# Moving a gating product from GpSimd to VectorE, and a convolution's residual into PSUM, in a four-layer kernel

## The chip, the core and the metric

The kernel runs on one core of a Trainium2 chip. The time is the device time of one execution in microseconds (us). Five engines work side by side, each through its own queue in order: TensorE (PE in the profile, its weight loads PEld), VectorE (DVE), ScalarE (ACT), GpSimd (POOL) and SyncE (SP), which here only issues DMAs. Before the change three runs took 3255.39, 3256.88 and 3258.67 us: the median is 3256.88 us.

## The reference

Four layers follow one another on an input x of 4 images, 128 channels and 64 x 64 pixels.

```python
# layer 0: attention over the 4096 pixels of an image
energy = einsum('bnd,bdm->bnm', q, k); attn = softmax(energy, -1)
x = gamma * einsum('bcj,bij->bci', v, attn) + x
# layer 1: two quantised 3x3 convolutions with seven taps each
out = act_quant(bn_eval(conv3x3(x, wq1)))            # clip to 0..1, 16 levels
x = act_quant(bn_eval(conv3x3(out, wq2)) + x)
# layer 2: Mamba over the pixels, 256 inner channels, 16 states
xh, z = split(x @ W_in); xh = silu(causal_conv_k2(xh))
h = exp(dt * A) * h + dt * B * xh                    # per pixel, channel and state
y = sum over states of h * C + xh * D
y = (y * silu(z)) @ W_out                            # the gating
x = silu(group_norm(y)) + x
# layer 3: attention with 64 channels, softmax(k q^T) v, projection, + x
```

## The kernel before, in words

Channels lie on the 128 partitions. An image's 4096 pixels are cut into pieces of 512 (8 rows); the first piece of the first image is halved, so there are 33 pieces, 31 of 512 pixels and 2 of 256. Image after image passes layer 0 (attention, mostly PE and ACT), layer 1 (`convolutions`), layer 2 (`preparation`, `decays`, `scans`, `additions`, `output`) and layer 3 (attention again). The eight attention stages run on PE and ACT while DVE works through the scans of other images. The last stage, layer 3 of the fourth image, can start only when the scans of that image are done.

**The scans.** For one state of a piece ACT computes the decay exp(dt A) into PSUM (line 1285, one instruction for each half of the 256 channels). For two states at a time DVE multiplies dt·x by B (line 1311, operands `ud` and `b_n`, both in SBUF), runs the recurrence for each state and half as one scan instruction (line 1331), and multiplies by C (line 1348, also two SBUF operands). POOL then adds each state's result to `y` (line 1359), 16 adds to a piece. When the sixteenth is done, POOL multiplies `y` by `sz` = silu(z) (line 1363), both halves in one instruction, and `mark("gated", g)` lets PE multiply by W_out (line 1168). `sz` is written by ACT (lines 1052 and 1082) and has one buffer.

**Who may run beside whom.** Some DVE instructions are marked `port=True` and passed through `held` (line 891). `behind` (line 894) makes each POOL add or gating wait for the last held DVE instruction before it in program order; that one is called its holder here. Scans aren't held, so an add runs beside the two scans that follow a line 1311 or a line 1348.

**The second convolution.** In `convolutions` (line 914) PE sums seven taps into a PSUM tile. ACT applies scale and offset and writes SBUF (line 973). DVE adds 15 times the layer's input from `xpad` (line 977, held), limits the sum to 0..15 (line 984, held), and rounds by adding and subtracting a large constant `MAGIC` while converting to 8 bits into `x1s` (line 987, held). PE reads `x1s` for the products of the Mamba layer.

**One small PSUM bank.** `gtile` (line 276) gives out a tile of one PSUM bank; its pool has one buffer. Convolutions, projections of the Mamba layer, transposes and small sums all use it in turn. An item of work marked `bank=True` takes it, and `release()` frees it.

**The order.** Each part of the work is a Python generator. Each `yield op(...)` names the engine, a planned time and what must be done before. The class `Order` (line 188) holds one chain for each letter, and the string `SCORE`, 9949 letters long, says which chain issues its next item. So the program order on every engine is written out by hand, letter by letter. The planned times have no part in running it.

Of the kernel before, what the change touches and what calls it, by code (L numbers as in the profile page):

```python
# [74 lines left out]
    "finish3": "CDEFGHIJ",  # L75
# [4 lines left out]
ittiiuccbvaauitatiaiswjaijaiiukuiviajkajiitkwtiikjijkikcuuisjbbibjkbbittikjjidkikuujiikjibbxcjik  # L80
xxkxbajijabjikkikjjiidxkjayyyykijyieeesejkibjseeiceeceeeekfjkffkijfikffkjjiifdxfjfffxkjxffffpffk
xiixpesfkjkfeffjenlnmlnnfmniinpekfellhmjfnnknenomjoifjkfinhmnlnnmjeifkdlijenpyneylnommjkkihlneyi
eefsnjojknnnflnlhmmffopnnnnfiinkynfkkjiyomlmhjnfpnoonnojlfiknpnjflfmfnonnsmfhkldffnoffkxxnnnxlol
mfppxxnehkfiinenfffejmnnjofekiehlneofmelnjmnnonnikejieneesjflkmeikohjmlnnijpnnijlnophmmnkfflkons
nnodiynijnnyppjmylflfhmkkinjoonnifjfnolflnnnommhnnkfpffkifnnnlnfmhmjokpgonlnnifngjllnfhmfonnnfmn
nikfjffylfmlhpyfmiiokfkdonnonnnnjofkfpfhfknjisljmijfnnonkkploinmnipjjkklnonomnfiikjjhinolkjdfimj
nxnikfxfxxlpnnkxfppjxmoxkkenehenmlijonijeelnmkniijpeeokenhjlnneeeiiemknojnjlfppfnhmkpiodnjinnjfo
kkflkmnnfkflinnmnijhjponppflfmknoniinjogfjklimjgijhnnlkfnokffmndypnpijffnyyfylkkpnyymynflhiejmff
onennokkffijffieejekhkmieelnijnfeenopkinejlmjkndiikjjnloihpneiknjmpnopnklkojpinmfnjikhklnnfomnne
oijflpiknfjkisjfpmdnxjlnmnnoxhpnoiffxjxkkpiljxmiffjnnogklxxmhiisknnojgffkgpennlfefkjifnemopnnejo  # L90
limhiennkjfnpejklnpmfofdiijelnfmkknfnhjoninifjflgnjmnkkijikkjplmpohnifinnonjjkklmnfdijonyffeeffe
ipheenkkjmlnnyykypiiyyojyjffkiijkkknejelopmnnnpmklninhjoiejiipjsdelkjnnompiiknelnhmnffonklnmonnf
fejjkppnfkifpilofmnhnnjjoekflmnzffknnggglpniokotzzzmitudenuxhnelneieeoivmittpfnufuhnmlnpiiwntpit
xxolununxxmfffnflxxmopneheoffffffinnnefeepfelnimtntponeveeesieelomuuniwneefijkhnliifnojjmnijpnln
pkhomiijnneeeejlpkknmnonpkiefelmeeopjnnhfkinijjlmknnkidijmkonlnnfkffsijohljimpnnfjkijkijnoeplenh
pnffmokipljnnoofnfkiimlgnjggkmnknfpnofdyphlnnyfikmfynyoyyjmylpnnonhfnkijjfpfkflmijnonnijlkijkmnn
ophijpkeiiljfkfnmekjonnfpffldmnpoehnnnijiffekifjfpklkjnmnkiikejofnlmphnonnjkiijkjefkofldxnmnijxx
xpnijhlmnkonkiikexjnxxlmonknsijikjjippnlfkjffmennfphijoinlfnmnoefkjlmnhnpopnnofffokidigfkglfmfgp
jnnjhnmfklepoekeiifnnjnpjkelonkimnnpffielojjmkfnffhinijknlonmkdynjeklneepeiyikyyeoyhnmjpnnpyjkif
ylnfoijmkkjneielnihjnkjmiinjjolnmeeeeonnffkfffkpiednppoijjeflkkhnmienenjifkmelpjnokkiijnknjiiljm  # L100
jnhonnklkdmxnpnoijinopjlnkxxxkfmnksxfxpiixhlnnkjmfjofinejnilnjohmnepenoopkfkiiffjlkmffgnkpngeefd
kglnjiiemonhnnepjmoljnkfnfelfkijnfmfnhokifipnnkjipjlmikjfjfkonnnlmfpnfonhkdlnnfeiijmyjeokknlipim
nkpnnojikjhjeenepoilijkjnmnpffiifkffnyyjkyykiydljhmnynkokijifjkklnesjemijonnpnilnmnpfeoekeenpjol
mkiinneknjljepneomkdnxffnepeiijkofxxmfplnxjnkenffxijiopkxxmlknjineljnijpnfkmifonejilkkgmnonnnooj
fgkfmlngeeippnsdelnjmnnpikfoeijfknifjijjfflekkinmonifkfnjklmnnojpffkfnlpiimnonnfjlkndmynjeeioeek
kjlymiyyispenynppkyjjoiikkfjynfffeefnjkfilnjeemneoenkiiljemnkepndkjomlniijhnnpofnkjkilisoenmnjkk
pneofjilmfipjnjhnlnkzfkfmfonnlfpenitkpthimdnxpuxunzxonffiilnvtitxxxiexolzzuumenwimentfitugnounfi
phgngipfgvttfloiggnmniuuoplwffffijnmonghiigjjlnnpknmfnfkoiifeljenmjnnpflhonekepiimfjopnkejlnknii
pkhjmijnjelnonmeeeinoggponffggeffikkfdggkggggggeejglgnjgnkgeeesmgknggeihijkkjlngpgiinokmejknpjlg
nghkpmdnyoiiejjgenijyilkyyykmnegeeynnyfokfijjijkpnkmlnniiheofknjoffjmlnppfinenoijlmknsjfhfnnkoio  # L110
igfdjkjfpmplngkffkgfniglfmhnieefnnjonjiikelekpmoenjnknjlmhoinnpnjifkklfjmopfiidnxnjxnlnmffnjkkox
hfpknpxxxpolmfixnjnijlenphkeomnknijnifjpffkffmiljknknofnpieojeidljhmnnnijeekkkoliijkjmknnnfiflij
jpmhkkeoknnpnildnjmnyioejepnelosypynkiiykyhjmyynkjinijlfkfmjfkffnnpoeeminphoilnkejnffmklnnfjoini
ejlghnjngmnkefoedipnepeoifgslmkfojekknnnpffmeiholjennienkjjemlnfipiojnffkkpnplfhomnjnknieffflkjd
iixnmnonpkjxlxxxnojkxmnxihijjlkefnkkmenonffiifjeeppfjfehknilmknpnionejjijkdlnoijmipnnokkijlifneh
mnnkjjkoeilmeiknkfppnnfjleejsonmnifhniokjjplnfkfmdyinepnijfopljkfyfmkyyhyiinlnfmjnpoyyjneeokgnkk
fgflmgnofhnnfnilimnnjkefpejieiojlmfknnnffhokpnjlmideppiojfkkfjifnnnlnmhjniojlnfmkkiijjkninliksfp
onohmpknnnjjlmokdpnnxfffffnpeikxxxkjijleijmnknhelijoffnexmninkjkijkopnmloijnkhnpnlopkxndmiinxene
jjlnkkiimhnjjkkponepiiflkjknomnenpfjmhfslnnfoknppiijjflkfmfdnynonifljhggmnonnooijikjelyyngyeymne
pikyfyfphlkffnomfnnnelnipofffjmpnjfffehkklnnmenioepneeijlkjnmnoeisijnflkjkidnomhpnneiejjolkfkknm  # L120
nffffkiijefejempepniiplokkhnejnnjezekeflpomknzznnlniimnhvonwliopdxnviminnfwlnfxfimznfhvopenlnfmo
infwxpfifenvhxospmlnnnoofxwlgmingjijpnxxliijgnnmnjhkkkkifofppnikjlkffnmofkipjlfkfnnnhfmnonkfijif
kplnjmokifnnjjkdloidimhjpjennnmelfnkkponkkkknopifjmlhijnfeeijpennfijfflkkkfeokijmnnkkiiddpnjkplj
mehkoiiennnjklpeekknjskmioniCljnhnjiiomnjnfflmnnCkkkokkpjkldpijenifmodhnfnnppjijklomknniienfplkk
fkjmknnhonojklnfiiemknpnjkfjlinhoimnnjppjofkkkfilnmddijnjglengkkkhmnfnonpokfkkflmfpnAiinnjejlehe
mnofnnoijffflmnniiffefkppkjCilkkCChfnCpmnonnooeCkkjjCidCdfgjmklfnnkfffkijijfenhlnkkkminopjepnelo
ikjfCksknDmDniipjkkkenjliioddknjkmpnnpkijlijkjnmkflkiionnmnnjjofkknfplmnnofifjieplnfpfmonnnkjifo
kkojflgfinifpgmkgjfflnmDnonDnnDDDiDjBddilnkkomnDkkklpkmpnojjfnnnfffiljmnifnkkiffoEkEppnjlmonnkkj
pkfflndiijEndikEomjkknknilpEmoEjpiEFjnnnkkkolnFijmnfffjDAffkkinjloiEnEpmfjpnEikknkjiidldmFFkojnn
jnkoklphFmnnnkkiFFiBfjlnFjkkmnFppiiojjlnnkkipjmoinffhknflfnomnkfpjfkdlmhnffioinnnojojlgdgiimnffk  # L130
gppkkjngklggknfpfiomhnjkjnnklnffmiiffnojklkjijmnpfpfFinnAfhofnkkloGGmnnnkddjlnphmofninGGjpplnikk
kkomGkGinGjkjlGmGhijijnnnggpokknfkffkiikfkgjiddlfjkmfHoGnnHnkjlnkoihmpjijnHniiHHkkHHBookflnmpnji
jlgHjmpHnnnohgngkkgggggggpggmgiglkkfkoknnifjfpjggnifidggodlmnfgjkkfnjgkhilgmpnfgpngknoHjfkgkknfo
# [54 lines left out]
class Order:  # L188
# [5 lines left out]
    def __init__(self):  # L194
        self.marks = set()
        self.chains, self.count = {}, {}
        self.locks = {True: None, "h": None}

    @staticmethod
    def op(engine, time, *needs, bank=False, **_):  # L200
        return needs, bank
# [1696 lines left out]
```

## Time and profile before

The profile is of one execution, whose own time was 3258.73 us; the instructions span 3256.9 us of it.

| | busy, us | share of the span |
|---|---|---|
| TensorE | 3075.6 | 94% |
| VectorE | 2942.3 | 90% |
| ScalarE | 2550.4 | 78% |
| GpSimd | 1298.7 | 40% |
| line 1363, gating on POOL, 33 instructions | 75.9 | 2.3% |
| line 987, second rounding on DVE, 33 instructions | 14.5 | 0.4% |

The mean granted TensorE clock was 0.983. In a line of the groups stand the source line, the engine and the operation, the tiles written and read, the shapes and the count; then the busy time in us and the mean duration of one in ns; and after the second bar the time that the engine sat idle just before these instructions, with what ended that time. Such a duration runs from an instruction's start to its end, and on DVE and ACT the next instruction can start some hundredths of a microsecond earlier. In a line of the timeline stand the start, the length, the engine, the line, the operation and, at xN, how many such instructions were merged.

### The profile page before, as it was taken

How to read it: one execution, taken by the hardware profiler on the slowest of the kernel's cores; microseconds unless marked ns; L12 is line 12 of the kernel's file. 1: busy time of each engine (PE TensorE's matmuls, PEld its weight loads, DVE VectorE, ACT ScalarE, POOL GpSimd, SP SyncE). 2: the span in 40 equal slices, each digit the busy share in tenths (PEclk: the TensorE clock that was granted, in tenths of full speed). 3: DMA queues.
4: the chain of work that ended last, by engine and by line, in shares of the span. 5: the costliest groups of instructions: out<-in, count | busy, mean ns of one | idle time of the engine just before them, and what ended most of it. 6: DMA issues, size and time to landing. Idle time of an engine off the chain costs nothing. (4 is left out here: it accounts for less than half of the span.)

```text
span 3256.9 us, 69082 instructions
## 1 busy us (share of the span) xinstructions
PE 3075.6 (94%) x29404; PEld 2260.7 (69%) x29404; DVE 2942.3 (90%) x2377; ACT 2550.4 (78%) x3734; POOL 1298.7 (40%) x582
## 2 busy tenths in 40 slices
PE   8989989999899999999898999999899999999998
PEld 7878858888688887555556878865566555565665
DVE  3699999999999999999999999999999999993554
ACT  5888878888788887888787888878888888875554
POOL 0244444444344444444444444444444444450000
PEclk9999999999999999999999999999999999999999
DMA  2233333233333334333333222233333333330000
GB/s 71 81 99 106 102 118 104 96 108 105 108 117 103 104 102 131 105 109 117 111 130 127 99 98 93 97 125 109 104 125 114 133 114 113 119 108 11 2 11 22
DMA packets 134878, 321.67 MB, mean 99 GB/s; under 512 B 44384, under 2 KB 55072, under 8 KB 134560
## 3 DMA queue, kind: packets, MB, share of 16 engines
q1 hardware_dynamic: 134272, 316.32, 28.9%
q8 instruction: 232, 3.80, 0.5%
q10 hardware_dynamic: 288, 0.85, 0.1%
q14 instruction: 86, 0.70, 0.1%
HBM read 300.35 MB, written 16.78 MB: 97 GB/s over the span
## 5 line engine op out<-in xcount | busy, mean ns | idle before, releaser
L1359 POOL TENSOR_TENSOR y<-y,hs 128x1024 f32<-128x1024 f32 (+1 forms) x528 | 1220.0, 2311 | 1569.1 <-DVE hs L1311 644.6
L659 ACT ACTIVATE p<-e 128x1024 f32<-128x1024 f32 x1024 | 1016.4, 1019 | 183.5 <-PE e L641 161.7
L1331 DVE TENSOR_TENSOR_SCAN hs<-da,hlast,hs 128x512 f32<-128x512 f32 (+1 forms) x928 | 1124.7, 1249 | 36.6 <-ACT da L1285 15.8
L723 PE MATMUL us<-v,p 128*128 128x129 f32 x8192 | 1012.9, 280 | 23.7 <-ACT us L780 11.2
L723 PEld LDWEIGHTS us<-v,p 128*128 128x128 f32 x8192 | 964.5, 194 | 81.4 <-ACT p L659 16.8
L1285 ACT ACTIVATE da<-dt,late 128x512 f32<-128x512 f32 (+1 forms) x1056 | 705.5, 677 | 303.4 <-DVE hs L1331 292.0
L1311 DVE TENSOR_TENSOR hs<-ud,b_n 128x2048 f32<-128x2048 f32 (+1 forms) x264 | 620.0, 2348 | 6.3 <-POOL y L1359 4.2
L1348 DVE TENSOR_TENSOR hs<-hs,c_n 128x2048 f32<-128x2048 f32 (+1 forms) x264 | 590.8, 2238 | 4.5 <-DMA c_n<-bc_d 2.3
L641 PE MATMUL e<-it,v 64*128 64x256 f32 x4096 | 531.6, 396 | 21.7 <-ACT p L659 21.3
L732 PE MATMUL us<-p,v 128*32 128x256 f32 x8192 | 501.8, 383 | 4.7 <-ACT p L659 4.1
L641 PEld LDWEIGHTS e<-it,v 64*128 64x128 f32 x4096 | 373.1, 188 | 162.4 <-issue 74.8
L732 PEld LDWEIGHTS us<-p,v 128*32 128x32 f32 x8192 | 246.2, 110 | 216.5 <-issue 53.3
L641 PE MATMUL e<-it,j 64*128 64x256 f32 x2048 | 208.8, 313 | 24.5 <-ACT p L659 19.3
L641 PEld LDWEIGHTS e<-it,j 64*128 64x128 f32 x2048 | 142.7, 186 | 88.0 <-ACT p L659 31.6
L751 PE MATMUL us<-p,ones 128*32 128x256 f32 x3072 | 202.6, 381 | 0.0
L681 DVE TENSOR_TENSOR acc<-p,acc 128x1024 f32<-128x1024 f32 x96 | 117.5, 1224 | 39.3 <-ACT p L659 32.5
L751 PEld LDWEIGHTS us<-p,ones 128*32 128x32 f32 x3072 | 96.1, 110 | 72.9 <-issue 13.2
L1331 DVE TENSOR_TENSOR_SCAN hs<-da,hs 128x512 f32<-128x512 f32 (+1 forms) x128 | 133.2, 1074 | 7.0 <-ACT da L1285 4.4
L1028 PEld LDWEIGHTS <-w 128*128 128x128 bf16 x594 | 53.1, 98 | 85.8 <-issue 43.9
L1028 PE MATMUL xh<-x,w 128*128 128x512 fp8e4 (+1 forms) x396 | 94.7, 375 | 14.0 <-ACT xc L1074 6.7
L1363 POOL TENSOR_TENSOR y<-y,sz 128x1024 f32<-128x1024 f32 (+1 forms) x33 | 75.9, 2301 | 71.4 <-DVE hs L1348 54.8
L681 DVE TENSOR_TENSOR acc<-p 128x1024 f32<-128x1024 f32 x16 | 19.6, 1224 | 83.1 <-PE ss L694 44.4
(173 smaller groups left out, 2563.6 us busy)
## 6 DMA issues: line engine op xcount, KB each, us to landing
b_n<-bc_d SPq DMA_DIRECT2D x256, 512.0 KB, 3.7
c_n<-bc_d SPq DMA_DIRECT2D x256, 512.0 KB, 3.7
x_in<-in_x SPq DMA_DIRECT2D x16, 512.0 KB, 6.1
xpad<-in_x SPq DMA_DIRECT2D x32, 256.0 KB, 4.6
x_d<-yo SPq DMA_DIRECT2D x24, 256.0 KB, 2.1
x_in<-x_d SPq DMA_DIRECT2D x12, 512.0 KB, 5.1
o<-x_d SPq DMA_DIRECT2D x24, 256.0 KB, 4.0
out<-o SPq DMA_DIRECT2D x24, 256.0 KB, 4.2
```

What stands on the lines that cost most here:

```text
L641: nc.tensor.matmul(e[h][:, k % 2, k // 4, :], lhsT=jts[s][row : row + D3, col : col + P], rhs=its[s][row : row + D3, c * CB : (c + 1) * CB ...
L659: nc.scalar.activation(p, es[t][h], AF.Exp)
L681: nc.vector.tensor_add(accs[k], ps[t, h], other)
L723: nc.tensor.matmul(us[:, r, 0:VP], lhsT=ps[t, h][:, k % 2, k // 4, r * P : (r + 1) * P], rhs=vts[s][:, 8 * q + k, :], start=q == 0 and k = ...
L732: nc.tensor.matmul(us[m : m + 32, 0, :], lhsT=vts[s][:, 8 * q + k, m % D3 : m % D3 + 32], rhs=ps[t, h][:, k % 2, k // 4, :], start=q == 0 ...
L751: nc.tensor.matmul(us[32 * m : 32 * m + 32, 1, :], lhsT=ones[:, 0:32], rhs=term, start=False, stop=q == NQ - 1 and k >= len(terms) - 4,)
L1028: nc.tensor.matmul(g, lhsT=w3[:, k // len(rhs), lhs[k % len(rhs)] : lhs[k % len(rhs)] + P], rhs=x[:, rhs[k % len(rhs)]], start=(k == 0), s ...
L1285: nc.scalar.activation(da, live["in", g][0][:, h, :], AF.Exp, scale=amat[:, h, n : n + 1])
L1311: held(nc.vector.tensor_mul(hs, live["in", g][1].unsqueeze(1).to_broadcast([P, 2, 2, T]), bcs.pop(("b", k)).unsqueeze(2).to_broadcast([P, ...
L1331: nc.vector.tensor_tensor_scan(hs[:, m % 2, h, :], das.pop((m, h)), hs[:, m % 2, h, :], hlast[:, n, h : h + 1] if index[g] else 0.0, ALU.mult,
L1348: nc.vector.tensor_mul(hs, hs, bcs.pop(("c", k))[:, a:b].unsqueeze(2).to_broadcast([P, b - a, 2, T]))
L1359: behind(nc.gpsimd.tensor_tensor(y, y, hs[:, m % 2], ALU.add))
```

## The change

The gating leaves POOL. A new chain `gate` copies silu(z) with ACT into the one PSUM bank, a half of the channels at a time, and DVE multiplies that half of `y` by it, in place. So a piece has two ACT copies and two DVE products in place of one POOL product, and the bank is used in turn by both halves.

In the second convolution ACT's scale and offset are written back into the PSUM tile. DVE adds the residual from there, no longer held, and frees the bank only then. The upper bound is joined with the addition of `MAGIC` in one DVE instruction. ACT subtracts `MAGIC` with a Relu, which is also the bound at zero, and converts to 8 bits. A constant tile for the offset is filled once by POOL.

The score is a new one of 10048 letters (132 more for the gating, 33 fewer for the additions), and `finish3` has five letters in place of eight. The class `Order` takes a mark `~` that sets a flag; the score has no such mark and nothing reads the flag.

```diff
-    "finish3": "CDEFGHIJ",
+    "finish3": "CDEFG",
+    "gate": "H",
 }
 SCORE = "".join(
...
+    magic = const.tile([P, 1], F32, tag="magic", name="magic")
+    nc.gpsimd.memset(magic, -MAGIC)
...
                 g = gtile("conv")[:, 0 : n * W]
                 conv(g, rpad, wint[1], a, range(7))
                 yield op("ACT", 0.2 + 0.58 * part, who=who)
+                nc.scalar.activation(g, g, AF.Identity, bias=b2, scale=s2)
+                yield op("DVE", 0.12 + 0.57 * part, who=who)
                 t = att.tile([P, TB], F32, tag="t", name="q2", bufs=1)[:, 0 : n * W]
-                nc.scalar.activation(t, g, AF.Identity, bias=b2, scale=s2)
+                nc.vector.scalar_tensor_tensor(
+                    img(t), rows_of(xpad, a, n), LEVELS, img(g), ALU.mult, ALU.add
+                )
                 release()
-                yield op("DVE", 0.12 + 0.57 * part, port=True, who=who)
-                held(
-                    nc.vector.scalar_tensor_tensor(
-                        img(t), rows_of(xpad, a, n), LEVELS, img(t), ALU.mult, ALU.add
-                    )
-                )
                 if (a + n) % ROWS == 0:
                     mark("taken", b, block)
                 yield op("DVE", 0.1 + 0.33 * part, port=True, who=who)
-                held(nc.vector.tensor_scalar(t, t, 0.0, LEVELS, ALU.max, ALU.min))
-                yield op("DVE", 0.1 + 0.33 * part, port=True, who=who)
-                held(
-                    nc.vector.tensor_scalar(
-                        x1s[b % 2][:, 1 + a * W : 1 + (a + n) * W],
-                        t,
-                        MAGIC,
-                        MAGIC,
-                        ALU.add,
-                        ALU.subtract,
-                        saturate=False,
-                    )
+                held(nc.vector.tensor_scalar(t, t, LEVELS, MAGIC, ALU.min, ALU.add))
+                yield op("ACT", 0.2 + 0.49 * part, who=who)
+                nc.scalar.activation(
+                    x1s[b % 2][:, 1 + a * W : 1 + (a + n) * W],
+                    t,
+                    AF.Relu,
+                    bias=magic,
+                    saturate=False,
                 )
                 mark("x1", b, c)
...
             mark("add", m)
             if n == DS - 1:
-                yield op("POOL", 0.1 + 2.3 * width(g) / TB, ("sz", g))
-                behind(nc.gpsimd.tensor_tensor(y, y, live.pop(("sz", g)), ALU.mult))
-                mark("gated", g)
+                order.add(gate(g, y))
+
+    def gate(g, y):
+        part = width(g) / TB
+        for h in range(2):
+            yield op("ACT", 0.2 + 0.4 * part, ("sz", g), bank=True)
+            sz = live.pop(("sz", g)) if h == 0 else sz
+            ps = gtile("gate")[:, 0 : width(g)]
+            nc.scalar.copy(ps, sz[:, h, :])
+            yield op("DVE", 0.12 + 0.57 * part)
+            nc.vector.tensor_mul(y[:, h, :], y[:, h, :], ps)
+            release()
+        mark("gated", g)
```

## The prediction, made before the result was known

> **What bounds the kernel now.** I read the page's busy times and slices first.
>
> ```profile
> span 3256.9 us, 69082 instructions
> PE 3075.6 (94%) x29404; PEld 2260.7 (69%) x29404; DVE 2942.3 (90%) x2377; ACT 2550.4 (78%) x3734; POOL 1298.7 (40%) x582
> ...
> DVE  3699999999999999999999999999999999993554
> ACT  5888878888788887888787888878888888875554
> POOL 0244444444344444444444444444444444450000
> ```
>
> VectorE (DVE) is full from the second to the 36th slice; the last four are the final attention, which TensorE (PE) fills. The table of stretches says how full:
>
> ```profile
> 1400.00:2000.00 600.00, 561.33 (x5437) 396.94 (x5434) 578.53 (x438) 488.89 (x716) 273.54 (x117) 0.97 0.33 112
> 2600.00:2900.00 300.00, 291.83 (x3582) 179.18 (x3582) 291.98 (x202) 245.04 (x366) 149.04 (x62) 1.00 0.34 116
> ```
>
> Columns: window, length, then PE, weight loads, DVE, ACT, POOL. Summed over 160 to 2900 us, DVE idles 69 us of 2740, PE 155, ACT some 490, most of it behind scans. So a microsecond added to DVE there moves the last scan, and with it the final attention. The groups give the prices:
>
> ```profile
> L1285 ACT ACTIVATE da<-dt,late 128x512 f32<-128x512 f32 (+1 forms) x1056 | 705.5, 677 | 303.4 <-DVE hs L1331 292.0 <-DVE dt L1144 8.2
> L1363 POOL TENSOR_TENSOR y<-y,sz 128x1024 f32<-128x1024 f32 (+1 forms) x33 | 75.9, 2301 | 71.4 <-DVE hs L1348 54.8 <-DVE x L987 4.3 <-DVE hs L1311 3.2
> L977 DVE SCALAR_TENSOR_TENSOR q<-xpad,q 128x512 f32<-128x512 f32 (+1 forms) x33 | 22.1, 670 | 1.0 <-ACT q L973 1.0
> L880 DVE TENSOR_TENSOR o<-o,o 128x512 f32<-128x512 f32 x24 | 16.1, 672 | 2.0 <-PE o L876 2.0
> L987 DVE TENSOR_SCALAR x<-q 128x512 fp8e4<-128x512 f32 (+1 forms) x33 | 14.5, 439 | 0.6
> ```
>
> Last the timeline of POOL, then of DVE, a few instructions after a gating:
>
> ```profile
> 1929.44 2.35 POOL L1359 TENSOR_TENSOR y<-y,hs 128x1024 f32<-128x1024 f32 x1 [2.57 <-DVE hs L1311]
> 1934.25 4.81 POOL L1359 TENSOR_TENSOR y<-y,hs 128x1024 f32<-128x1024 f32 x2 [2.45 <-DVE hs L1348]
> ```
> ```profile
> 1931.84 2.27 DVE L1348 TENSOR_TENSOR hs<-hs,c_n 128x2048 f32<-128x2048 f32 x1
> 1934.02 2.45 DVE L1331 TENSOR_TENSOR_SCAN hs<-da,hlast,hs 128x512 f32<-128x512 f32 x2
> 1936.48 0.69 DVE L1184 BATCH_NORM_STATS2 stats<-yo 128x6 f32<-128x512 f32 x1
> 1937.09 4.12 DVE L1311 TENSOR_TENSOR hs<-ud,b_n 128x2048 f32<-128x2048 f32 x1
> ```
>
> One add (2.36) fits beside two scans (2.45). Here two adds ran behind one holder, until 1939.06, and L1311, which reads two SBUF operands, took 4.12 us in place of 2.28. A piece has 16 adds and 16 such places; the gating is a seventeenth POOL instruction, so about one place per piece gets two. Instruction by instruction: 127 full-width L1311 overlap an add and average 2.545 us, the 120 that overlap none 2.282; 64 L1348 average 2.387 against 2.268. That is 33.4 + 7.6 us; with smaller rows some 50 us of DVE's busy time is waiting for POOL, 24.6 of it in 23 places with two adds and 20.0 spread over 364 places with one.
>
> **The change, part by part.** A DVE price is the step from one start to the next in back-to-back work, about 0.08 us under the duration (L1184 above: 0.69 long, 0.61 step).
>
> *Gating, DVE.* Added: 66 multiplies, SBUF by PSUM: 62 of 128x512, 4 of half. Nearest row L880, same shape and operands: step 0.583. 62 x 0.583 + 4 x 0.35 = 37.5 us, all on the full engine. Bounds: L880 below, L977's 0.669 (two SBUF operands) above: 37.5 to 43. The trace shows seven L880 wholly under a POOL add at 0.665 us against 0.688 alone, so these don't collide.
>
> [...]
>
> *Second convolution, DVE.* The two bounds and the rounding were two tensor_scalars (L984, L987); now one. L987 goes: 31 x 0.361 + 2 x 0.2 = -11.6. L977's step 0.669 becomes the PSUM form, as L819 (0.650): -0.6. L984 turns into L950's operation (0.413 against 0.345; part of that is overlap): 0 to -2.2, take -1.0. DVE's sum: 37.5 - 11.6 - 0.6 - 1.0 = **+24.3**.
>
> *POOL.* 33 gatings go, 75.9 us. POOL is 60% idle, so that time alone is worth nothing; what counts is the seventeenth place. I followed both scores letter by letter: at full width the old one puts two POOL instructions behind one holder some 30 times, the new one 10 times. Of the 10, four have a wide DVE instruction beside the scans, which covers the second add; four have two short ones and cost 0.95 each, the mean of such places now; two have scans alone, some 2.2 (4.80 of adds less 2.45 and the start). That is 8 us against 24.6: -16.6. Places with one add beside nothing but two scans fall from 379 to 305: 20.0 x 74/379 = -4. L1311's idle time behind POOL, 4.3 in the stretch, I leave. Next in line on DVE are then the scans that wait for ACT's decay, 14.5 us in the stretch. Relief **-21**; bounds 0 (other adds collide instead) and -54 (all 50 + 4.3 goes).
>
> *ACT.* Added: 66 copies SBUF to PSUM, 62 x 0.626 (L1285's step, same direction) + 4 x 0.41 = 40.5, and 33 Relus at L952's 0.521, 16.8. L973 now writes PSUM: no row, bounds ±0.1 each, 0. The 57 us lie in ACT's 490 idle us, mostly waits for a scan; uncovered, they cost 57.
>
> *Waits.* Each multiply waits for its copy, and behind it on DVE stand scans. In the score the first multiply stands at least two scans behind the holder of the piece's last add, except in the last piece, so POOL isn't waited for. For the copy, DVE's idle time behind ACT in the long stretch gives L1139 0.08 us each (2.7/33), L533 0.46 (6.0/13): 5 to 30 us for 66. I take 0.1, nearer L1139, since 35 multiplies have another DVE instruction between copy and multiply: **+6.6**. The rounding's Relu is read by PE, a piece ahead of the scans: 0; uncovered, 33 x 0.6.
>
> *The one bank "g".* It holds every small matmul result. From first matmul to last reader it is taken 1697 of 2740 us. Copy and multiply add 66 x 1.3 = 86, the longer second convolution 33 x 0.65 = 21. Behind a matmul that waits for it PE queues energies and products. Cover: PE's 155 idle us and inputs a piece ahead. I take 0; 36 turns are followed by another user than the gating, so up to 36 x 1.3 = 47 on PE.
>
> *Order.* At every 48th step of the scan chain the new score has issued within four as many products, energies and exponentials as the old (finish3 moves a little more). Before the first scan PE has 85 items in place of 86, and exp, silu, ln and sqrt tables change 151 times against 149 (+2.6 at 1.28 on ACT, covered). So the head (first scan at 105 us, PE 31 to 40 of 40 busy) and the final attention keep their length: 0, ±8 for local shuffles. *Tail.* The last gating, 2938.0 to 2940.4 on POOL, becomes multiply, copy, multiply: 0.67 + 0.63 + 0.67 + two hand-overs, 2.1 to 2.4: 0. The constant's memset lies in the idle head of POOL.
>
> **Sum.** The profiled execution took 3258.7 (span 3256.9), 1.9 above the median. 3258.7 + 24.3 - 21 + 6.6 = 3268.6; less 1.9, **3267 us**, 0.3% slower.
>
> **Rivals.**
> 1. *The seventeenth place was worth more (faster).* If nearly all overlap goes, -45, and hand-overs cost nothing: 24.3 - 45 = -21, 3236; at two thirds of that, 3247. For it: a back-to-back pair stands some instructions after most gatings. Against: 20 of the 50 us sit in places with one add, which stay. It decides once relief exceeds 24.3 plus the waits.
> 2. *DVE stalls behind ACT's copy or bank g.* At L533's 0.46 per multiply 30 us: 3291. For it: in 31 cases copy and multiply are neighbours in the score, and a late copy holds DVE outright. Against: L1139, L977 and L1184 hardly wait for ACT.
> 3. *DVE's load doesn't set the end.* From 2600 to 2900 PE is 97% busy too; then relief and load both vanish in PE's order: 3257. Against: PE idles 155 us earlier.
>
> **How the numbers follow.** This kernel's measurement tells about 0.2%, 6.5 us: 3250.4 to 3263.4. Forecast 0.42 (own range 3257 to 3278: 0.30 slower, 0.12 same); rival 1 0.30 (0.28 faster); rival 2 0.18, all slower; rival 3 0.10 (0.06 same, the rest split evenly). Faster 0.30, same 0.20, slower 0.50. The range runs from two thirds into rival 1 (3241) to rival 2's price (3292).
>
> **What would show it.** Right: POOL near 1223 us; DVE busy up only a few us although 66 multiplies at about 0.67 and no L987 appear; L1311's mean, 2348 ns now, near 2270 (20 us over 264); few 4.8 us pairs on POOL. Wrong on the slow side: idle time before the multiply put down to ACT's copy above 10 us, or PE waiting for it at conv, z or xh. Wrong on the fast side: L1311 and L1348 both at 2.27 at full width, and DVE's idle time below 69 us in its long stretch.

## The result: faster by 0.7%, and the profile after

The changed kernel took 3233.82 us (median of four runs, 3233.17 to 3235.41), the kernel before 3256.14 (four runs, 3255.30 to 3258.67). The ratio is 0.9931, with an interval of 0.9914 to 0.9948. The forecast, 3267 us, had the wrong sign. The time also lies under the range, 7 us below its lower end. Rival 1, at 3236, came nearest. The profiled execution took 3233.38 us (span 3230.2), with a granted clock of 0.989.

Busy times and slices on the page of the kernel after:

```profile
span 3230.2 us, 69145 instructions
...
PE 3049.1 (94%) x29404; PEld 2251.7 (70%) x29404; DVE 2928.3 (91%) x2410; ACT 2602.4 (81%) x3835; POOL 1218.6 (38%) x550
...
DVE  3699999999999999999999999999999999993554
ACT  5888888888888888888787888888888888875554
POOL 0234434444434444444434444444444444450000
```

DVE has 33 instructions more than before (2410 against 2377), among them 66 products that cost 43 us. Even so its busy time is 14.0 us lower. So all its other work takes 57.2 us less than before, 14.5 of it the second rounding, which has left DVE. The shape of the slices is the old one: a full DVE, then the last attention stage.

Table of stretches, kernel before, then after (window, length, then PE, weight loads, DVE, ACT, POOL):

```profile
160.00:2900.00 2740.00, 2584.96 (x24098) 1910.46 (x24101) 2670.87 (x2022) 2244.40 (x3297) 1252.49 (x539) 0.98 0.33 111
```
```profile
160.00:2900.00 2740.00, 2584.13 (x24469) 1914.19 (x24466) 2685.35 (x2074) 2313.41 (x3422) 1190.81 (x515) 0.99 0.34 112
1400.00:2000.00 600.00, 557.95 (x5445) 398.85 (x5446) 585.67 (x453) 502.14 (x744) 259.11 (x111) 0.99 0.34 112
2600.00:2900.00 300.00, 292.47 (x3628) 180.42 (x3620) 295.65 (x211) 248.59 (x368) 140.44 (x60) 1.00 0.34 114
```

DVE's idle time from 160 to 2900 us is now 2740 - 2685.4 = 54.6 us; it was 69.1. In 1400 to 2000 it is 14.3 against 21.5, and in 2600 to 2900 it is 4.4 against 8.0.

Groups of the kernel before, then of the kernel after (busy time and mean ns of one, then the idle time just before them and what ended it):

```profile
L1311 DVE TENSOR_TENSOR hs<-ud,b_n 128x2048 f32<-128x2048 f32 (+1 forms) x264 | 620.0, 2348 | 6.3 <-POOL y L1359 4.2
L1348 DVE TENSOR_TENSOR hs<-hs,c_n 128x2048 f32<-128x2048 f32 (+1 forms) x264 | 590.8, 2238 | 4.5 <-DMA c_n<-bc_d 2.3 <-ACT hlast L1295 2.2
```

```profile
L1363 POOL TENSOR_TENSOR y<-y,hs 128x1024 f32<-128x1024 f32 (+1 forms) x528 | 1215.9, 2303 | 1688.6 <-DVE hs L1315 703.3 <-DVE hs L1352 452.4 <-DVE q L960 172.7
...
L1315 DVE TENSOR_TENSOR hs<-ud,b_n 128x2048 f32<-128x2048 f32 (+1 forms) x264 | 596.8, 2261 | 6.2 <-POOL y L1363 3.6 <-DMA b_n<-bc_d 0.2
L1352 DVE TENSOR_TENSOR hs<-hs,c_n 128x2048 f32<-128x2048 f32 (+1 forms) x264 | 585.7, 2218 | 0.7 <-DMA c_n<-bc_d 0.7
...
L1376 DVE TENSOR_TENSOR y<-y,gate 128x512 f32<-128x512 f32 (+1 forms) x66 | 43.2, 654 | 5.6 <-POOL y L1363 4.4 <-ACT gate L1374 1.1
...
L1374 ACT COPY gate<-sz 128x512 f32<-128x512 f32 (+1 forms) x66 | 37.8, 573 | 19.7 <-DVE y L1376 15.7 <-DVE rall L860 2.2 <-DVE q L985 1.5
...
L994 ACT ACTIVATE x<-q,magic 128x512 fp8e4<-128x512 f32 (+1 forms) x33 | 23.4, 709 | 8.1 <-DVE q L992 7.9
...
L985 DVE SCALAR_TENSOR_TENSOR q<-xpad,conv 128x512 f32<-128x512 f32 (+1 forms) x33 | 21.4, 649 | 2.2 <-ACT conv L982 2.2
```

L1315 is the line 1311 of before and L1352 its 1348. The mean of L1315 has fallen from 2348 ns to 2261, with the narrow ones of the half pieces counted in; at full width it fell from 2417 to 2327, and that of L1352 from 2299 to 2283. The product L1376 waited 1.1 us in all for its copy; its other wait, 4.4 us for POOL, is in the last piece. The copy itself, L1374, waited 15.7 us for the product before it, because both halves use the same bank.

Timeline of the kernel after around one product, first POOL, then DVE (start, length):

```profile
1381.70 2.35 POOL L1363 TENSOR_TENSOR y<-y,hs 128x1024 f32<-128x1024 f32 x1 [2.42 <-DVE hs L1352]
1386.85 2.37 POOL L1363 TENSOR_TENSOR y<-y,hs 128x1024 f32<-128x1024 f32 x1 [2.80 <-DVE hs L1315]
```
```profile
1379.30 2.27 DVE L1352 TENSOR_TENSOR hs<-hs,c_n 128x2048 f32<-128x2048 f32 x1
1381.48 0.68 DVE L1376 TENSOR_TENSOR y<-y,gate 128x512 f32<-128x512 f32 x1
1382.08 2.45 DVE L1335 TENSOR_TENSOR_SCAN hs<-da,hlast,hs 128x512 f32<-128x512 f32 x2
1384.44 2.27 DVE L1315 TENSOR_TENSOR hs<-ud,b_n 128x2048 f32<-128x2048 f32 x1
```

The add starts at 1381.70, just after the C product, and ends at 1384.05. Beside it lie the gating product and two scans. The next L1315 comes at 1384.44, when POOL is done, and takes 2.27 us; the 163 of full width that overlap no add take 2.278 on the mean. Before the change a L1311 behind two adds took 4.12.

**Where the time went.** I went through DVE's instructions from the first dt·x·B product to the end of the last C product, in both traces. This is called the stretch below. Busy time counts no overlap twice.

| part of the stretch, us | before | after | difference | predicted |
|---|---|---|---|---|
| gating products | 0 | 36.8 | +36.8 | +37.5 |
| second rounding on DVE | 12.8 | 0 | -12.8 | -11.6 |
| residual and bounds | | | -1.3 | -1.6 |
| dt·x·B products | 602.5 | 578.8 | -23.7 | |
| C products | 569.5 | 564.0 | -5.5 | |
| small GroupNorm instructions | | | -5.4 | |
| all others | | | -4.5 | |
| *the last four: less waiting for POOL* | | | *-39.1* | *-21* |
| DVE idle | 77.1 | 62.0 | -15.0 | +6.6 |
| length of the stretch | 2829.4 | 2798.0 | -31.4 | +9.9 |

The first dt·x·B product starts 2.5 us later, and what follows the last C product is 2.3 longer. That leaves -26.6 of the span. So two terms of the sum failed: the relief is nearly twice as large, and DVE's idle time fell where I had it rise.

### The profile page after: what moved, and what is told of

The parts are those of the page before. It is cut to its first block, busy times and chain, and to the rows that moved or that the text cites. A ratio compares the mean times of both kernels' runs of the same rounds, so it can differ in the third digit from the quotient of the medians.

```text
span 3230.2 us, 69145 instructions
## 1 busy us (share of the span) xinstructions
PE 3049.1 (94%) x29404; PEld 2251.7 (70%) x29404; DVE 2928.3 (91%) x2410; ACT 2602.4 (81%) x3835; POOL 1218.6 (38%) x550
## 3 DMA queue, kind: packets, MB, share of 16 engines
q1 hardware_dynamic: 134272, 316.32, 29.9%
## 5 line engine op out<-in xcount | busy, mean ns | idle before, releaser
L1315 DVE TENSOR_TENSOR hs<-ud,b_n 128x2048 f32<-128x2048 f32 (+1 forms) x264 | 596.8, 2261 | 6.2 <-POOL y L1363 3.6
L1352 DVE TENSOR_TENSOR hs<-hs,c_n 128x2048 f32<-128x2048 f32 (+1 forms) x264 | 585.7, 2218 | 0.7 <-DMA c_n<-bc_d 0.7
L651 PE MATMUL e<-it,v 64*128 64x256 f32 x4096 | 521.8, 392 | 12.2 <-ACT p L669 11.7
L651 PEld LDWEIGHTS e<-it,j 64*128 64x128 f32 x2048 | 141.5, 185 | 81.5 <-ACT p L669 31.6
L691 DVE TENSOR_TENSOR acc<-p,acc 128x1024 f32<-128x1024 f32 x96 | 117.6, 1225 | 40.1 <-ACT p L669 33.1
L1122 PE MATMUL dt_ps<-xd,late 128*128 128x256 f32 (+1 forms) x264 | 70.8, 391 | 8.3 <-ACT sp L1134 4.9
```

Source lines behind the costliest of these rows:

```text
L651: nc.tensor.matmul(e[h][:, k % 2, k // 4, :], lhsT=jts[s][row : row + D3, col : col + P], rhs=its[s][row : row + D3, c * CB : (c + 1) * CB ...
L691: nc.vector.tensor_add(accs[k], ps[t, h], other)
L1315: held(nc.vector.tensor_mul(hs, live["in", g][1].unsqueeze(1).to_broadcast([P, 2, 2, T]), bcs.pop(("b", k)).unsqueeze(2).to_broadcast([P, ...
L1352: nc.vector.tensor_mul(hs, hs, bcs.pop(("c", k))[:, a:b].unsqueeze(2).to_broadcast([P, b - a, 2, T]))
```

## The experiments

The kernel before was run beside each group of runs; its medians there were 3258.27, 3259.54 and 3259.39 us. Busy and idle are DVE's in the stretch, as in the table above. Spans and these two columns are of the profiled execution. The runs are on several chips, on which the median of the kernel before differs by up to 3.4 us; a difference of some us between two runs of the table, after among them, is no more certain than that.

| run | median, us | ratio to before (interval) | span | busy | idle |
|---|---|---|---|---|---|
| before | 3256.14 | | 3256.9 | 2752.4 | 77.1 |
| after | 3233.82 | 0.9931 (0.9914 to 0.9948) | 3230.2 | 2736.0 | 62.0 |
| conv_old_order | 3299.97 | 1.0132 (1.0115 to 1.0148) | 3298.4 | 2739.6 | 127.8 |
| gate_old_order | 3364.37 | 1.0329 (1.0312 to 1.0347) | 3362.5 | 2757.8 | 167.1 |
| both_old_order | 3406.68 | 1.0464 (1.0446 to 1.0482) | 3400.4 | 2746.0 | 217.4 |
| conv_old_later_relu | 3277.17 | 1.0047 (1.0030 to 1.0064) | 3278.1 | 2741.2 | 106.0 |
| both_old_later | 3380.06 | 1.0368 (1.0350 to 1.0385) | 3378.6 | 2745.3 | 198.2 |
| new_order_alone | 3322.73 | 1.0197 (1.0180 to 1.0214) | 3317.1 | 2799.8 | 85.9 |
| conv_gate_on_pool_new_order | 3274.23 | 1.0052 (1.0035 to 1.0069) | 3271.0 | 2752.2 | 84.4 |
| no_gating_old_order | 3227.05 | 0.9902 (0.9886 to 0.9919) | 3225.9 | 2714.4 | 81.5 |
| gating_left_out | 3209.57 | 0.9842 (0.9826 to 0.9859) | 3208.8 | 2707.8 | 68.7 |
| product_from_sbuf | 3247.99 | 0.9963 (0.9949 to 0.9977) | 3247.9 | 2752.8 | 62.8 |
| conv_undone_new_order | 3284.13 | 1.0076 (1.0059 to 1.0092) | 3282.5 | 2782.1 | 67.8 |
| rounding_back_on_dve | 3263.41 | 1.0014 (1.0004 to 1.0023) | 3263.2 | 2766.7 | 63.8 |

No run with the whole computation was faster than the changed kernel.

### Each part alone, in the old order

The first question was which part brought the gain. I took each part into the kernel before and kept its score, with as few letters changed as the parts need. conv_old_order has the second convolution of after. Because the bank is freed one step later there, four letters of the convolution chain stand earlier.

```diff
+                nc.scalar.activation(g, g, AF.Identity, bias=b2, scale=s2)
...
+                    img(t), rows_of(xpad, a, n), LEVELS, img(g), ALU.mult, ALU.add
...
+                held(nc.vector.tensor_scalar(t, t, LEVELS, MAGIC, ALU.min, ALU.add))
...
+                    AF.Relu,
```

> The old score with the second convolution's change alone; gating stays on POOL. Four letters of the convolution chain stand earlier, because the longer hold of the one PSUM bank would otherwise overlap its next user. If DVE's load sets the end: the rounding that leaves DVE is worth 12.8 us and the PSUM residual 0.7, so 3256 - 13.5 = 3243. If the gain of the changed kernel lies in its new score: 3256, no change. If the longer hold of the bank costs: above 3258.

Measured: 3299.97 us, ratio 1.0132 (1.0115 to 1.0148). The first two values were missed by over 40 us; the third, above 3258 if the longer hold of the bank costs, is met, though most of the time has another cause. DVE's busy time behaved as the sum says (-12.8), but its idle time rose by 50.7. The chain that ended these waits begins on ACT. Waits of ACT in conv_old_order (waiting line, releaser, us in total, times, longest):

```profile
ACT da L1287 <- DVE hs L1333: 235.1, 304, 2.8
ACT p L667 <- PE e L649: 190.5, 169, 5.1
ACT x L992 <- DVE q L990: 40.1, 16, 4.8
```

Waits of DVE in the same run:

```profile
DVE hs L1333 <- ACT da L1287: 43.2, 46, 5.7
```

L992 is the new Relu. In the old order it stands where DVE's rounding stood, so ACT's queue reaches it before DVE has done L990. For 40.1 us in 16 places ACT stands still there, with decays queued behind it. The scans' wait for those decays is 43.2 us here. In the kernel before it was 20.3:

```profile
DVE hs L1331 <- ACT da L1285: 20.3, 29, 1.7
```

gate_old_order has only the gating of after, on the chain `gate`, with its four letters a few places apart behind the last addition of a piece, and the letters of the additions moved so that each holder has one.

```diff
-                yield op("POOL", 0.1 + 2.3 * width(g) / TB, ("sz", g))
-                behind(nc.gpsimd.tensor_tensor(y, y, live.pop(("sz", g)), ALU.mult))
-                mark("gated", g)
+                order.add(gate(g, y))
```

> The old score with the gating's change alone. The adds of POOL are laid out anew by one rule, one add behind each holder where it fits, and the copies and products stand at the first places where the bank is free, two scans behind the piece's last add; all else keeps the old order. Theory 'seventeenth instruction': the products add 36.8 us to DVE, the pairs of adds go (24.6 us in the trace of before, about 4 left), and DVE's small instructions and single adds lose some 10 more: 3256 + 36.8 - 31 = 3262, between 3254 and 3268. Theory 'new score': without it the products cost their full price, 3256 + 36.8 - 0 to 5 = 3288 to 3293.

both_old_order joins the two.

> Both changes of the arithmetic under the old score, adds laid out as in the run with the gating alone, nothing searched. 'Seventeenth instruction' with the convolution's saving: 3256 + 36.8 - 13.5 - 31 = 3248, between 3240 and 3256, so at most half of the 22 us gain is the new score's. 'New score': 3256 + 36.8 - 13.5 = 3279, and the score's search is worth the whole gain and more.

Measured: 3364.37 us, 1.0329 (1.0312 to 1.0347), and 3406.68 us, 1.0464 (1.0446 to 1.0482). Every value expected was missed, by over 70 us in the first run and by over 125 in the second. In gate_old_order the sum on DVE's busy time again held: +5.4, which is +39.8 of products and -34.4 of relief. Idle time rose by 90.0, and in both_old_order by 140.3. In gate_old_order this is how ACT waited:

```profile
ACT da L1295 <- DVE hs L1341: 162.7, 217, 3.2
ACT gate L1380 <- DVE y L1382: 80.8, 30, 4.9
```

This is the second copy of a piece, waiting for the bank that the first half's product hasn't freed. And PE waited for the same bank:

```profile
PE conv L916 <- DVE y L1382: 38.4, 5, 9.9
PE z L1038 <- DVE y L1382: 29.9, 8, 9.3
```

So rival 2's mechanism (DVE behind ACT and the bank) exists, and where the copies and products stand badly it costs far more than the 30 us that I gave it. Part of that size is my placing of the four letters, which no search went over.

### The same with the stalls moved

If those waits at the head of ACT's queue are the cause, moving only these letters must give the time back. conv_old_later_relu moves the Relu's letter later in 21 of 33 cases, until some 2.4 us of planned DVE work stand between it and the step before it, or until the next user of its result or of its tile.

> The convolution's change alone under the old score, as before, but in 21 of 33 pieces the letter of the new Relu stands two to four DVE instructions later, so that ACT meets it when DVE's limit-and-add is done. Theory 'head of ACT's queue': the 51 us that DVE idled more came from ACT waiting at that Relu (40.1 us in 16 waits) with decays queued behind; they go to some 10 to 20, and the time falls from 3300 to 3253 to 3270, ACT's wait for line 990 below 10 us. Rival 'the bank is held longer': the Relu has no part in that, 3290 to 3300.

Measured: 3277.17 us, 1.0047 (1.0030 to 1.0064): 22.8 us less than conv_old_order, with nothing else changed. The wait of L992 fell from 40.1 us to 6.9. So that stall is shown, and its price is over half of the 41.7 us that the convolution's change lost in this order. The time lies between the two values expected, 3253 to 3270 and, for a bank held longer, 3290 to 3300: other waits stayed. Waits of ACT, then of PE:

```profile
ACT sz L1054 <- PE z L1030: 24.2, 17, 5.1
```
```profile
PE z L1030 <- DVE q L983: 14.3, 4, 5.5
PE sc L849 <- DVE q L983: 8.4, 2, 4.8
```

L983 is the residual, which frees the bank. PE waited for it as long in conv_old_order (13.8 and 8.3 us), so the longer hold of the bank may well be part of what is left; no run takes it away alone. The scans still waited 40.2 us for decays.

both_old_later does the same to both parts, with the second copy also later.

> Both changes under the old score, adds one to a holder, the Relu later as in the run beside it, and the second copy of a gating later too: at least 2.4 us of DVE work behind the first product where the next reader of the gated piece allows it. 'Head of ACT's queue': the 81 us that ACT stood at the copy go to some 30 and the Relu's 40 to under 10, so 3407 falls by 60 to 110, to 3297 to 3347. If only a search of the whole order helps: above 3380.

Measured: 3380.06 us, 1.0368 (1.0350 to 1.0385), only 26.6 us under both_old_order, where I had expected some 60 or more; it is just at the "above 3380" of the case in which only a new order of everything helps. Waits of ACT, first both_old_order, then both_old_later:

```profile
ACT gate L1374 <- DVE y L1376: 69.6, 30, 4.9
ACT sz L1056 <- PE z L1032: 35.9, 34, 2.5
ACT q L957 <- PE conv L916: 31.8, 19, 5.9
```
```profile
ACT sz L1056 <- PE z L1032: 58.4, 38, 4.9
ACT q L957 <- PE conv L916: 40.8, 20, 8.7
...
ACT gate L1374 <- DVE y L1376: 21.5, 16, 4.9
```

The copy's own wait fell by 48.1 us, but a copy that stands later holds the one bank later. PE then waits for it (z 43.5 to 64.8 us), and ACT waits for PE. The stall only changed its place. Moving these letters wasn't enough to bring this arithmetic into the old order; in the new one the same two instructions wait 15.7 and 7.9 us, and DVE is idle for 62.0 us in place of 198.2.

### The new order without the new arithmetic

new_order_alone turns the question round: the old code under the new score, with a POOL gating at the place of the first addition letter after a piece's sixteenth, the gating letters removed and one more addition letter for each piece.

```diff
-                order.add(gate(g, y))
+                yield op("POOL", 0.1 + 2.3 * width(g) / TB, ("sz", g))
+                behind(nc.gpsimd.tensor_tensor(y, y, live.pop(("sz", g)), ALU.mult))
+                mark("gated", g)
```

> The old arithmetic in both places under the new score, gating on POOL placed as in the run with the convolution's change alone. If the new score were the gain: below 3256. From the runs so far: gating on POOL in this order 3274, convolution undone +50 (more held instructions among the adds): 3300 to 3330.

Measured: 3322.73 us, 1.0197 (1.0180 to 1.0214), as the theory of an order that needs its arithmetic had it. Group of the dt·x·B products there:

```profile
L1319 DVE TENSOR_TENSOR hs<-ud,b_n 128x2048 f32<-128x2048 f32 (+1 forms) x264 | 627.1, 2375 | 27.1 <-POOL y L1367 24.5
```

They are longer (2375 ns) and on top of that wait 24.5 us for adds. The likely reason is that held instructions of the convolution and the seventeenth POOL instruction come where the new order has no place for them. But one number goes the other way. DVE's idle time is longer in all (85.9 us against 77.1), yet its idle time before all other instructions is 85.9 - 27.1 = 58.8 us, where before had 70.9 and after has 55.8. So if the waits before the dt·x·B products are left aside, some 12 of the 15.0 us of idle time that the change saved are also saved by the new order under the old arithmetic.

### What the gating on POOL cost

no_gating_old_order is the kernel before without its gating; the additions are spread as in gate_old_order.

```diff
-                behind(nc.gpsimd.tensor_tensor(y, y, live.pop(("sz", g)), ALU.mult))
```

> The kernel before without its gating (the output leaves out the factor silu(z)), POOL's adds laid out one to a holder, all other letters of the old score. It prices the seventeenth POOL instruction where it stood. 'Seventeenth instruction': DVE gets back what the gating with both changes alone gave back in the old order, 34 us of waits for POOL: 3258 - 34 = 3224, between 3218 and 3232. If POOL's pairs cost only what stands in their own places (24.6 us and 3): 3230. If the old order's idle time grows into the space: 3235 to 3258.

Measured: 3227.05 us, 0.9902 (0.9886 to 0.9919); expected was 3224, within 3218 to 3232. Groups:

```profile
L1321 DVE TENSOR_TENSOR hs<-ud,b_n 128x2048 f32<-128x2048 f32 (+1 forms) x264 | 597.2, 2262 | 7.7 <-POOL y L1369 5.2 <-DMA b_n<-bc_d 0.3
L1358 DVE TENSOR_TENSOR hs<-hs,c_n 128x2048 f32<-128x2048 f32 (+1 forms) x264 | 584.4, 2214 | 2.5 <-ACT hlast L1305 1.6 <-DMA c_n<-bc_d 0.8
```

2262 and 2214 ns are the means of after as well (2261, 2218). On an engine that is 60% idle, 33 instructions of 2.3 us, with the old spread of the adds, cost the kernel 31.0 us of span (3256.9 to 3225.9), and all of it as longer DVE instructions: busy fell by 38.0, idle rose by 4.4. Since the run also moved most letters of the adds, it doesn't part the gating from their old spread; no run has the new spread with the gating on POOL in the old order.

conv_gate_on_pool_new_order asks the same within the new kernel: after, with the gating back on POOL by the edit of new_order_alone.

> The changed kernel with the gating put back on POOL as one instruction, its copies and products left out of the score, and the seventeenth POOL instruction placed within the next nine adds, where the stretch without held DVE instructions is longest. 'Seventeenth instruction': DVE loses 36.8 us of products and gains pairs again in about 33 places at 0.7 to 2 us, 35 to 60 us: 3233 to 3258, L1311's mean back to 2340 ns or more. 'New score' (gain independent of the gating): 3234 - 36.8 = 3197 to 3205.

Measured: 3274.23 us, 1.0052 (1.0035 to 1.0069), 40.4 us above after and 16 above the upper value expected. Against after, 36.8 us of products go, but DVE's busy time rises by 16.2 and its idle time by 22.4:

```profile
L1313 DVE TENSOR_TENSOR hs<-ud,b_n 128x2048 f32<-128x2048 f32 (+1 forms) x264 | 620.3, 2350 | 20.3 <-POOL y L1361 16.7 <-DMA b_n<-bc_d 0.7
```

2350 ns is the mean of before again, and the wait for POOL is 16.7 us in place of 3.6. So the price of the gating on POOL depends on the order: here it is 62.2 us of span over the same kernel without a gating (gating_left_out, below).

### What the gating on DVE costs

gating_left_out takes copies and products out of the kernel after.

```diff
-            ps = gtile("gate")[:, 0 : width(g)]
-            nc.scalar.copy(ps, sz[:, h, :])
-            nc.vector.tensor_mul(y[:, h, :], y[:, h, :], ps)
```

> The changed kernel without the gating: no copies, no products, so the output leaves out the factor silu(z); score and all else kept. It prices the new products and copies where they stand. If DVE's load sets the end: -36.8 - 1.1: 3196, between 3190 and 3203. If PE, 97% busy from 2600 us on, is as much a bound: 3210 to 3225.

Measured: 3209.57 us, 0.9842 (0.9826 to 0.9859). The span is 21.4 us below after's. Busy time falls by 28.2: the products' 36.8, less 6.9 that L1315 gains in length (2261 to 2287 ns), probably since some adds have lost the product that lay beside them. Idle time rises by 6.7. The time is 7 us above the value for a bound by DVE's load (3190 to 3203) and just below the one for a PE that is as much a bound (3210 to 3225). So it doesn't decide between the two, but it does refute rival 3 as it stood, by which relief and load both vanish: 28.2 us off DVE's load moved the end by 21.4.

product_from_sbuf asks what the detour over PSUM is worth: the product reads silu(z) where it is, without copy or bank.

```diff
-            ps = gtile("gate")[:, 0 : width(g)]
-            nc.scalar.copy(ps, sz[:, h, :])
-            nc.vector.tensor_mul(y[:, h, :], y[:, h, :], ps)
+            nc.vector.tensor_mul(y[:, h, :], y[:, h, :], sz[:, h, :])
```

> The changed kernel with silu(z) read from SBUF by the same two products, at the same places, no copies and no bank. 'PSUM keeps the products out of POOL's way': DVE's 66 products then wait for adds that are under way, 31 to 46 of them overlap one, at 0.3 to 1.5 us: 3234 + 10 to 50 = 3244 to 3284. 'Copies and bank are the price of the gating': ACT saves 40 us and the bank 86, the time falls to 3215 to 3230.

Measured: 3247.99 us, 0.9963 (0.9949 to 0.9977), 14.2 us above after; the theory that PSUM keeps the product out of POOL's way had 3244 to 3284, and the one in which copies and bank are a cost 3215 to 3230.

```profile
L1374 DVE TENSOR_TENSOR y<-y,sz 128x512 f32<-128x512 f32 (+1 forms) x66 | 61.2, 927 | 4.4 <-POOL y L1363 4.4
```

The same product takes 927 ns in place of 654, because it now meets the adds. Of the 62 at full width 46 overlap an add in either kernel: from SBUF these take 1059 ns on the mean, from PSUM 671. The 16 that overlap none take 672 and 670, so SBUF is no slower by itself. In the stretch, products cost 54.6 us in place of 36.8: +17.8, the whole difference in span (17.7). Idle time is 62.8 against 62.0, though the copies, the waits for them and 66 turns of the bank are gone. So in the new order these cost DVE no idle time that shows.

### The convolution in the new order

conv_undone_new_order is after with the convolution of before: residual, bounds and rounding held on DVE.

```diff
-                held(nc.vector.tensor_scalar(t, t, LEVELS, MAGIC, ALU.min, ALU.add))
+                held(nc.vector.tensor_scalar(t, t, 0.0, LEVELS, ALU.max, ALU.min))
...
+                        MAGIC,
+                        MAGIC,
+                        ALU.add,
+                        ALU.subtract,
```

> The changed kernel with the second convolution as it was: ACT writes SBUF, the bank is free earlier, DVE adds the residual from SBUF, limits and rounds; the letters are those of the new score, the rounding on DVE where the Relu's letter is. If DVE's load sets the end: +12.8 for the rounding, +0.7 for the residual, a few us for held instructions that single adds now run into: 3234 + 15 = 3249, between 3245 and 3256. If the order fitted to the change is what counts: another 10 to 40 us of DVE idle time, 3256 to 3285.

Measured: 3284.13 us, 1.0076 (1.0059 to 1.0092), 50 us above after. That is the upper end of the second value, but not by its way, which was idle time: this rose only by 5.8, and busy time by 46.1. Groups:

```profile
L1321 DVE TENSOR_TENSOR hs<-ud,b_n 128x2048 f32<-128x2048 f32 (+1 forms) x264 | 602.8, 2284 | 11.1 <-POOL y L1369 8.6 <-DMA b_n<-bc_d 0.3
L1358 DVE TENSOR_TENSOR hs<-hs,c_n 128x2048 f32<-128x2048 f32 (+1 forms) x264 | 600.3, 2274 | 1.3 <-DMA c_n<-bc_d 1.3
...
L987 DVE SCALAR_TENSOR_TENSOR q<-xpad,q 128x512 f32<-128x512 f32 (+1 forms) x33 | 27.1, 821 | 2.2 <-ACT q L983 2.2
L997 DVE TENSOR_SCALAR x<-q 128x512 fp8e4<-128x512 f32 (+1 forms) x33 | 17.5, 529 | 0.2
```

The instruction itself costs 15.0 us in the stretch. The C products have grown by 14.6 (2218 to 2274 ns), the residual from 649 to 821 ns, the dt·x·B products by 6.2. These are held instructions. My reading is that each one more cuts a place between two holders in two, and that an add of 2.36 us doesn't fit into the halves. In the old order the same change freed little beside its own time (conv_old_order: dt·x·B products -1.5 us, C products -1.4), so this price belongs to the new order.

rounding_back_on_dve takes only the last step back: the residual stays in PSUM, but DVE subtracts MAGIC and bounds at zero, held.

```diff
-                yield op("ACT", 0.2 + 0.49 * part, who=who)
-                nc.scalar.activation(
-                    x1s[b % 2][:, 1 + a * W : 1 + (a + n) * W],
-                    t,
-                    AF.Relu,
-                    bias=magic,
+                yield op("DVE", 0.1 + 0.33 * part, port=True, who=who)
+                held(
+                    nc.vector.tensor_scalar(
...
+                        MAGIC,
+                        0.0,
+                        ALU.subtract,
+                        ALU.max,
```

> The changed kernel with the last step of the second convolution on DVE: the residual stays in PSUM and not held, but subtracting the constant and the bound at zero are a held tensor_scalar at the Relu's letter. Undoing both halves cost 50 us, 20 in instructions and 26 in waits for POOL. If holders that cut up the adds' places are the cause, and both held instructions share in it: +13 for the instruction and 8 to 15 of waits, 3255 to 3262. If the residual alone did it: 3247. If the rounding alone did it: 3270 to 3280.

Measured: 3263.41 us, 1.0014 (1.0004 to 1.0023), just above the 3255 to 3262 of the theory of holders, and 30 us above after.

```profile
L1356 DVE TENSOR_TENSOR hs<-hs,c_n 128x2048 f32<-128x2048 f32 (+1 forms) x264 | 599.0, 2269 | 1.8 <-ACT h L541 1.0 <-DMA c_n<-bc_d 0.8
...
L995 DVE TENSOR_SCALAR x<-q 128x512 fp8e4<-128x512 f32 (+1 forms) x33 | 15.5, 468 | 0.2
```

The 33 instructions add 12.9 us of busy time. The C products behind them add 13.4 more, and the dt·x·B products and others 4.4. One held instruction for each piece, 0.39 us of busy time, costs over twice that. No run has it without the mark, so it isn't shown how much of the 18 us lies in the marking as held, which makes an add wait for it, and how much in the instruction itself.

### The pieces put together

By spans, the steps from before to after are: before 3256.9; without the gating, old order 3225.9; the new convolution and the new order, still without gating, 3208.8; with the gating on DVE 3230.2. By these, the gating on POOL with the old spread of the adds cost 31.0 us, on DVE it costs 21.4, and its move is worth 9.6; the convolution together with the new order is worth 17.1. The split is rough. By the ratios to the kernel before, each taken on its own chip, the four numbers are some 32, 29, 3 and 20 us.

## Why the prediction was wrong

**Relief from POOL (failed: -21 predicted, -39.1 measured).** The mechanism was right and its size was wrong. I counted letters, saw that ten pairs of POOL instructions would remain of some 30, and took 24.6 us down to 8, and 20.0 us in places with one add down to 16. Sorted in the same way, the trace after has 5.2 us and 12.8. That gives -26.6 in place of -20.6. The rest lies where I hadn't looked: -5.4 in GroupNorm's small instructions, and some 7 in half pieces and other groups. Most of this relief needs neither the new order nor the new convolution: gate_old_order, with the adds spread anew, already has -34.4. The argument against rival 1, "20 of the 50 us sit in places with one add, which stay", was the weak one: these places fell from 364 to 292, by a fifth as counted, but those that stay also cost less, 44 ns each on the mean in place of 55.

**Waits (failed: +6.6 predicted, -15.0 measured for all idle time).** The products wait 1.1 us for their copies, below even my lower bound of 5. I had priced the wait by lines that stood where the old order put them. The larger error is in the term "order": I compared how many products, energies and exponentials each score had issued at every 48th scan, found them equal within four, and gave 0. That tells about supply over long distances. What DVE waits for is decided within a few letters: whether a decay, a Relu or a copy reaches the head of ACT's queue before or after its input is there. In the stretch DVE's waits of over 0.15 us for ACT fell from 35.1 us to 24.8, and those for PE from 4.9 to 1.8. new_order_alone, with the old arithmetic, has 26.8 and 3.2. So most of this gain comes with the order itself; which letters bring it stays open.

**The Relu and the copies on ACT, "0" (right in number, wrong in argument).** I gave 0 because the Relu is read a piece ahead and ACT has idle time. The reader of a result is not the one who pays. Behind a Relu that waits stand decays, and behind these the scans: in the old order this cost at least the 22.8 us that later letters gave back. In the new order the Relu waits 7.9 us.

**The bank, "0" (right here).** product_from_sbuf takes away its 66 turns and saves DVE no idle time. In the old order PE waits for the same bank 38.4 and 29.9 us, so the 47 us on PE that I gave as the upper end (36 turns at 1.3 us) wasn't one.

**What held.** The products: +36.8 against +37.5. Their mean step is 0.589 us against 0.583 from line 880. Their duration, 670 ns on the mean at full width, is close to that of line 880 (672); the 36.8 us follow from the step. Beside no add the product took 672 ns from SBUF and 670 from PSUM. The rounding: -12.8 against -11.6. Residual and bounds: -1.3 against -1.6. POOL's busy time: 1218.6 against 1223. Head, tail and last stage: +2.5, +2.3 and, for the last stage from its first exponential on, 278.3 us against 277.7. Two more of the signs named came: dt·x·B products near 2270 ns, and under 10 us of idle time before the products. Of the two signs named for the fast side, DVE idle for less than 69 us came (54.6). Both wide products at 2.27 us at full width did not: C products came close (2.283), dt·x·B products stayed at 2.327, since some 85 of 248 still overlap an add.

**The sum with measured terms.** 36.8 - 12.8 - 1.3 - 39.1 - 15.0 + 2.5 + 2.3 = -26.6 of the span. The time outside the span grew by 1.3 us (1.8 to 3.2), which gives the 25.3 us between the two profiled executions. Rival 1 was stated with -45 of relief and no waits, 3236 us: the time was right within 3 us, partly by luck. Its relief was too large (-45 against -39.1), and the idle time that fell, which it didn't foresee, more than made up for it. Some numbers of the rivals don't fit together: two thirds of the way to rival 1 is 3247, as it says there, and not the 3241 of the range, and rival 2's price comes to 3290 by its own sum, not 3291 or 3292.

**What stays open.** The order and the arithmetic can't be told apart fully: against the kernel before, with the old arithmetic the new order is 2% slower, with the new arithmetic the old order is 4.6% slower. The last figure holds for my placing of the letters; an old order fitted to the gating alone wasn't tried. PE's granted clock is higher after (0.989 against 0.983), and its busy time 26.5 us lower for as many matmuls. That doesn't decide the time: gating_left_out and no_gating_old_order ran at 0.985 and 0.986 and were faster than after. But no run tells what part of the 15.0 us of idle time it has.

## What to carry to other kernels

Price an instruction on an idle engine by what it collides with: here 76 us of GpSimd work, on an engine busy for 40% of the time, cost some 31 us on VectorE with the spread of adds that it had, and 62 us in the new order: it was the seventeenth user of sixteen places. An operand brought into PSUM on an engine with room can be worth its copy: here the copies took 37.8 us of ScalarE, and beside an add the product took 671 ns on the mean in place of 1059 from SBUF, 14.2 us of the kernel's time. When work moves to another in-order engine, look first at what is queued behind it there at the moment when its input may be late (in conv_old_order a Relu waited 40.1 us with decays queued behind it), and expect that the order has to be laid out anew before the move pays: here both changes in the old order, as I placed their letters, were 4.6% slower.

## What the hardware showed that was not expected

In the kernel before, a VectorE instruction on a single column was held up twice beside a GpSimd add, for 2.22 and 2.21 us, nearly the 2.36 us of the add. Timeline of the kernel before, POOL, then DVE:

```profile
880.59 4.80 POOL L1359 TENSOR_TENSOR y<-y,hs 128x1024 f32<-128x1024 f32 x2 [4.20 <-DVE hs L1348]
```
```profile
882.99 0.16 DVE L1202 TENSOR_TENSOR gd<-gd 128x1 f32<-128x1 f32 x1
883.18 2.22 DVE L1203 TENSOR_TENSOR gd<-gd,mv 128x1 f32<-128x1 f32 x1
885.33 2.33 DVE L1331 TENSOR_TENSOR_SCAN hs<-da,hs 128x512 f32<-128x512 f32 x2
```

L1203 adds two columns of 128 numbers, which takes 0.16 us in two of the four images. Here it lasts until 885.40, and the second of the two adds ends at 885.38 (the line gives both adds as one, 880.59 + 4.80). L1202 started at 882.99, between the first add's end at 882.94 and the second one's start at 883.02, and wasn't held up. In the third image L1203 starts at 2285.53 and lasts until 2287.74, and the add beside it ends at 2287.72. So I read the 2.22 us as a wait to the end of the add: the 128 numbers alone take 0.16.

The other one is how much the place of an operand decides beside these adds: where they overlap an add, 671 ns on the mean for the full-width product from PSUM and 1059 for the same product from SBUF, measured in two kernels with the same order.
